# Four-layer graph network on one core: the order of the work around pairs 1 to 3, and where theta's third part is made

## Chip, cores and metric

The kernel runs on one core of one Trainium2 chip. The metric is the device time of one execution in microseconds (us). A core has a matrix engine (TensorE, here PE), a vector engine (VectorE, DVE), an activation engine (ScalarE, ACT), a general engine (GpSimd, POOL) and a queue that issues transfers (SyncE, SP). Each of the engines works through its own instructions in the order in which the program names them, and waits at an instruction until what that one reads is ready; whatever stands behind it waits too.

## What is computed

The input x has 32 batches of 512 nodes with 128 features, and adj is a 512 x 512 matrix. Four layers follow one another; each normalises x over the features, takes the positive part h and adds its result to x. The part of the reference that the change touches is layer 0, and in layer 1 the matrix Theta1:

```python
h = jnp.maximum(_layernorm(x, axis=-1), 0.0)
# layer 0
h0 = jnp.einsum('bnf,fg->bng', h, W[0])
h1 = jnp.einsum('bnf,fg->bng', h, W[1])
A = softmax(where(adj > 0, vals, NEG), axis=1)
out = jnp.einsum('ij,bjg->big', A * M, h0) + jnp.einsum('ij,bjg->big', A * (1.0 - M), h1)
x = x + out + bias                       # M is the identity
# layer 1: hops of h over adj, stacked, times Theta1
x = x + relu(stack([h, h1, h2, h1, h2]) @ Theta1 + bias)
```

Layer 2 has two products with a squared adj, and layer 3 is an attention over the nodes. Neither is touched.

## The kernel before

Batches are worked in 16 pairs, q = 0 to 15. A pair's x is one tile of 128 rows by 2 batches by 4 node blocks by 128 features. For layer 0 each pair goes through these steps:

- **Statistics.** Four `bn_stats` on DVE give mean and variance. There are two ways to a scale `rs` and a shift `sh` from there. `early_stats` (L217) makes them with four small operations on POOL, one of which is a power of -1/2 (L235). `stats_steps` (L239) makes a square root on ACT (L254), a reciprocal on DVE (L256) and two small operations on POOL (L258, L259). `stats_of_two` (L265) does the second for two pairs at once. Pairs 0 to 2 use the first way, pair 3 (`ln3`, L784) and later ones the second.
- **h.** Eight activations on ACT (`normed_steps`, L308), one for each batch and node block.
- **Turning h**, so that features lie on the rows. For pairs 0 to 2 PE transposes it (L330, and `turn_first` L607 for pair 0) and ACT copies it out (L333, L611). From pair 3 on, DVE transposes blocks of 32 (L348), and SP issues four writes to memory (L355) and one read back (L357), `hT`.
- **Diagonal.** `diagonal_of` (L805) multiplies the turned h by A's diagonal on POOL, two operations `hd` (L752). `own_sums` (L811) multiplies `hd` by W[0] on PE, 16 matmuls (L817).
- **Projection.** `project_steps` (L461) multiplies the turned h by W[1] on PE, 16 matmuls (L446), and splits the result into three parts: `g_high` on ACT (L468), `g_low` on DVE (L470), `g_mid` on POOL for the first batch (L474) and on DVE for the second (L472).
- **Product.** `mixed` (L820) multiplies a part of g by the same part of the off-diagonal A, eight matmuls (L824); three parts for each of two halves of the rows, 48 in a pair. `added` (L829) adds the sums to x on DVE; `bias` (L450) adds the bias on POOL.

All of PE, DVE, ACT and POOL follow the program order of the source; the schedule is written by hand. Many helpers are generators, and `go(steps, n)` (L477) runs the next n steps of one, so that its pieces can be laid between others. PSUM has eight banks that the tiles named by `bank` share.

Before the rounds stands a front part (to L738), which makes A by a softmax over rows: `later_rows` and `value_rows` on PE, `softmax_rows` (L680) on DVE and ACT, `scaled_rows` on ACT and POOL, and then A's three parts `att_high`, `att_low` and `att_mid` in two halves (L372 to L390). `first_sums` (L836) then does pair 0's sums and leads in pairs 1 to 3, and `round0(q)` (L886) is one pair's round: own sums of pair q, diagonals and projection of pair q + 1, statistics of pairs q - 1 (for layer 1) and q + 5, h of pair q + 4, turn of pair q + 3.

In `first_sums` the order around pair 1's diagonals is this: own sums of pair 0, h of pair 2, projection of pair 1 with its three parts, the last part of pair 0's product, and only then the diagonals of pair 1.

In layer 1, `fixed_parts` (L416) splits two blocks of theta into a high, a low and a middle part (L418 to L421); the middle part and the subtraction before it are on POOL. `split_up` (L971) splits h of a batch into parts through `moving_parts` (L410), whose low part is on POOL (L413) and whose middle part is on DVE (L414).

Of the kernel before, what the change touches and what calls it, by code (L numbers as in the profile page):

```python
# [9 lines left out]
F32 = mybir.dt.float32  # L10
# [3 lines left out]
AF = mybir.ActivationFunctionType  # L14
# [15 lines left out]
def kernel(  # L30
# [186 lines left out]
    def early_stats(q, *groups):  # L217

        st = stats.tile([P, NT, 2, 3], F32, tag="bn", name=f"bn_{q}", bufs=3)
        sd = stats.tile([P, NT, 2], F32, tag="sd", name=f"sd_{q}", bufs=2)  # L220
        rs = stats.tile([P, NT, 2], F32, tag="rs", name=f"rs_{q}")
        sh = stats.tile([P, NT, 2], F32, tag="sh", name=f"sh_{q}")
        shift[q] = sh.rearrange("p k e -> p (k e)")
        scale[q] = rs.rearrange("p k e -> p (k e)")
        for first, end in groups:
            for k in range(first, end):
                b, t = divmod(2 * k, NT)
                nc.vector.bn_stats(st[:, k].rearrange("p e s -> p (e s)"),
                                   xt[q][:, b, t : t + 2, :].rearrange("p t f -> p f t"))
                yield  # L230
            half = slice(first, end)
            nc.gpsimd.tensor_scalar(sd[:, half], st[:, half, :, 2], 1.0 / D, EPS, OP.mult, OP.add)
            nc.gpsimd.tensor_scalar(sh[:, half], st[:, half, :, 1], -1.0, None, OP.mult)
            yield
            nc.gpsimd.tensor_tensor(rs[:, half], sd[:, half], minus_half[:, half], OP.pow)  # L235
            nc.gpsimd.tensor_mul(sh[:, half], sh[:, half], rs[:, half])  # L236
            yield
# [239 lines left out]
    def go(steps, n=99):  # L477
        for _ in range(n):
            if next(steps, steps) is steps:
                return  # L480
# [63 lines left out]
    for t in range(NT):  # L544
        scores[t] = bank(f"p_later_{t}")
        nc.tensor.matmul(scores[t], ident16, m[:, t, :], start=True, stop=False)
    early = [early_stats(0, (0, 2), (2, 4)), early_stats(1, (0, 4)), early_stats(2, (0, 4))]
    go(early[0], 2)
    middle = prep.tile([P, NT], F32, name="middle")
    nc.vector.tensor_sub(middle, above, pi[:, :NT])  # L550
# [56 lines left out]
    def turn_first(b):  # L607
        p = bank(f"p_hT0_0_{b}")
        for t in range(NT):
            nc.tensor.transpose(p[:, blk(t)], h[0][:, b, t, :], ident)  # L610
        nc.scalar.copy(hT[0][:, :, b, :].rearrange("p b (a c) -> p b a c", c=QR), crossed(p))  # L611
# [56 lines left out]
    def later_rows(t):  # L668
        for kk in range(NK):
            nc.tensor.matmul(scores[t], at_row[:, kk, blk(t)], at_col[:, kk, :], start=False, stop=(kk == NK - 1))  # L670

    def value_rows(t):
        pv = bank(f"p_val_{t}")
        for kk in range(NK):
            for i in range(3):
                nc.tensor.matmul(pv, at_row[:, kk, blk(t)], at_part[:, i, kk, :], start=(kk == 0 and i == 0),
                                 stop=(kk == NK - 1 and i == 2))
        scores[t] = scores[t], pv

    def softmax_rows(t, between=lambda: None):  # L680
        ph, pv = scores[t]
        u = us[t]
        nc.vector.scalar_tensor_tensor(u, ph, elastn, att[:, t, :], OP.mult, OP.add)
        between()
        nc.vector.tensor_tensor_reduce(u, pv, u, 1.0, 3.0e38, OP.add, OP.min, least[:, t : t + 1])
        nc.scalar.activation(u, u, AF.Exp, bias=least[:, t : t + 1], scale=-1.0,
                             accum_out=total[:, t : t + 1])

    def inverse(t):
        nc.vector.reciprocal(total[:, t : t + 1], total[:, t : t + 1])  # L690
# [14 lines left out]
    softmax_rows(0)  # L705
    go(project[0][0])
    later_rows(2)
    value_rows(1)
    softmax_rows(1, lambda: inverse(0))
    scaled_rows(0)  # L710
    go(early[1], 1)
    later_rows(3)
    value_rows(2)
    turn_first(1)
    value_rows(3)

    def inverted(t):
# [5 lines left out]
    next(project[0][1])  # L723
    softmax_rows(3, lambda: inverted(2))
    next(project[0][1])
    go(early[1], 1)
    inverse(3)
    pt = [[bank(f"p_attT_{half}_{j}") for j in range(2)] for half in range(2)]
    transpose_rows(0)
# [1 line left out]
    att_high(0, 0, False)  # L731
    att_high(1, 0, True)
    scaled_rows(3)
    go(early[1], 1)
    go(project[0][1])
    go(early[1])
    att_low(0)
# [43 lines left out]
            yield  # L781

    ahead = {q: stats_steps(q, apart=True) for q in (4, 5)}
    ln3 = stats_steps(3, apart=True)  # L784
    own, turning, hd, adiag = {}, {}, {}, []
    sums_ahead = late_parts()

# [17 lines left out]
    def diagonal_of(q, b):  # L805
        hd[q, b] = straight(turned_of(q), b, adiag[0], f"hd_{q}_{b}")
# [4 lines left out]
    def own_sums(q, ps, first):  # L811


        for I, p in enumerate(ps):
            for i in range(2):
                for b in range(2):
                    nc.tensor.matmul(p[:, (2 * i + b) * D : (2 * i + b + 1) * D], hd[q, b][:, blk(2 * I + i)], w0[:, 0, :],  # L817
                                     start=(first and i == 0 and b == 0), stop=not first, skip_group_check=True)
# [17 lines left out]
    def first_sums():  # L836


        adiag.append(region0.tile([P, N], F32, name="adiag", bufs=1))
        ps = opened_sums(0)  # L840
        mixed(0, 0, ps[0], 0, True)
        transpose_rows(2)
        transpose_rows(3)
        p_adiag = bank("p_adiag")
        for t in range(NT):
            nc.tensor.matmul(p_adiag[:, blk(t)], ones, diag[:, t, :], start=True, stop=True)
        att_high(0, 1, True)
        att_high(1, 1, True)
        nc.scalar.copy(adiag[0], p_adiag)
        diagonal_of(0, 0)  # L850
        diagonal_of(0, 1)
        go(normal[1])
        mixed(0, 0, ps[0], 1, True)
        mixed(0, 0, ps[0], 2, True)
        mixed(0, 1, ps[1], 0, True)
        att_low(1)
        mixed(0, 1, ps[1], 1, True)
        go(early[2])
        att_mid(1)
        next(turned[1])  # L860
        go(turned[1])
        own_sums(0, ps, False)
        go(normal[2])
        next(project[1])
        go(project[1])
        mixed(0, 1, ps[1], 2, True)
        diagonal_of(1, 0)
        diagonal_of(1, 1)
        begun[1] = opened_sums(1)
        own_sums(1, begun[1], True)  # L870
        bias(1)
        for I in range(2):
            added(0, I, ps[I])
        next(turned[2])
        go(ln3)
        go(turned[2])
        normalise(3)
        diagonal_of(2, 0)
        diagonal_of(2, 1)
        go(ahead[4], NT)  # L880
        go(turn(3))
        go(ahead[4])
# [3 lines left out]
    def round0(q):  # L886

        more = q + 1 < NQ
        nothing = iter(())
        both = stats_of_two(q - 1, q + 5) if q + 5 < NQ else stats_steps(q - 1, apart=True)  # L890
        ps = begun.pop(q, None)
        if ps is None:
            ps = opened_sums(q)
            own_sums(q, ps, True)
        normal_of = normals.pop(q + 3, nothing)
        go(normal_of)
        go(both, NT)
        if more:
            if q > 1:
                diagonal_of(q + 1, 0)  # L900
                diagonal_of(q + 1, 1)
            steps = projection(q + 1)
            if q != 2:
                next(steps)
                if q > 2:
                    bias(q + 1)
                go(steps)
        if q + 5 >= NQ:
            go(both)
        if q == 1:  # L910
            bias(2)
            normalise(4)
            go(ahead[5])
            h[5] = normed_tile(5)
            normals[5] = normed_steps(5, h[5])
        elif q + 4 < NQ:
            h[q + 4] = normed_tile(q + 4)
            normals[q + 4] = normed_steps(q + 4, h[q + 4])
            go(normals[q + 4], NT)
        if q >= 5:  # L920
            go(sums_ahead, 1)
        for part in range(3):
            mixed(q, 0, ps[0], part, False)
        if q + 3 < NQ:
            go(turn(q + 3))
        if q == 2:
            go(steps)
            bias(q + 1)
        go(both, NT + 1)
        added(q, 0, ps[0])  # L930
        go(both)
        if q in (3, 4):
            next(squares)
            next(squares)
        if q == 5:
            go(squares)
        for part in range(3):
            mixed(q, 1, ps[1], part, False)
        added(q, 1, ps[1])
        if q == NQ - 1:  # L940
            own[q] = stats_steps(q)
        if q % 2 and q // 2 + NQ // 4 < NQ // 2:
            loads(q // 2 + NQ // 4)

    def layer1(more, square):
# [84 lines left out]
        yield  # L1030
        pair = small_tile("th_high", F32R), small_tile("th_low", F32R)
        th_parts = pair[0][:, : 2 * D], pair[0][:, 2 * D :], pair[1][:, : 2 * D]
        fixed_parts(th[:, 0:2, :].rearrange("p k f -> p (k f)"), *th_parts)
        split_up(0, 0)
        split_up(0, 1)
        split_up(1, 0)
        normalised(2)
# [519 lines left out]
```

## Time and profile before

| what | us |
|---|---|
| median of 3 runs | 885.37 (885.09 to 885.38) |
| profiled execution, whole time | 884.78 |
| its span, first to last instruction | 883.0 |
| PE busy from 0 to 20, 20 to 40, 40 to 60 | 16.64, 17.56, 16.19 |
| PE busy from 60 to 120 | 60.00 |
| PE busy from 120 to 200, 200 to 270 | 79.70, 69.61 |
| PE busy from 270 to 600, 600 to 883 | 330.00, 279.06 |
| DVE and POOL busy from 66 to 110 | 40.09, 40.52 |

In lines of the profile, L12 is line 12 of the source. A line of a timeline has the start, the duration, the engine, the line, the operation, and what it writes and reads; several of the same kind are drawn together (x8). A line of the waits has who waited for whom, then the total in us, how often, and the longest. The mean clock that PE was granted is 0.998 of full.

### The profile page before, as it was taken

The page shows a single profiled execution, that of the slowest core. Times are in us where ns is not written, and L with a number is a line of the kernel's source. Part 1 is how long each engine was busy: PE and PEld are TensorE (multiplying, and loading weights), DVE is VectorE, ACT ScalarE, POOL GpSimd, SP SyncE. Part 2 cuts the span into 40 slices and gives each one's busy share as a digit, 9 for nine tenths or more (in the row PEclk, how much of TensorE's full clock was granted, in tenths as well). Part 3 has the DMA queues.
Part 4 walks back from the last instruction along what each step waited for, and adds up shares of the span by engine and source line. Part 5 has one row for each costly group of instructions (what it writes and reads, how often), then busy time and mean ns, then how long its engine had stood idle before and what let it go on. Part 6 is the DMA issues. An engine that isn't in the chain of part 4 may idle for free.

```text
span 883.0 us, 16282 instructions
## 1 busy us (share of the span) xinstructions
PE 868.8 (98%) x5528; PEld 771.6 (87%) x5528; DVE 700.5 (79%) x1412; ACT 576.7 (65%) x1282; POOL 607.4 (69%) x625
## 2 busy tenths in 40 slices
PE   8799999999999999999999999999999999999998
PEld 4699999988888888888888888888889888899987
DVE  7769876568687787788778888888789789988875
ACT  5765565356555655556666888875688778766674
POOL 6659988767677767867776566565376766677664
PEclk9999999999999999999999999999999999999999
DMA  9137664312322213122332445455445555545442
GB/s 257 34 103 208 193 190 120 96 49 72 98 70 72 73 48 96 49 69 75 97 112 80 120 123 143 140 146 148 137 120 144 156 155 159 149 143 148 120 108 85
DMA packets 107684, 103.91 MB, mean 118 GB/s; under 512 B 9552, under 2 KB 94160, under 8 KB 107600
## 3 DMA queue, kind: packets, MB, share of 16 engines
q1 hardware_dynamic: 107312, 102.34, 40.7%
q8 instruction: 44, 0.72, 0.4%
q10 hardware_dynamic: 288, 0.52, 0.2%
q14 instruction: 40, 0.33, 0.1%
HBM read 53.02 MB, written 49.81 MB: 116 GB/s over the span
## 4 chain that ended last, share of the span: by engine, by line
PE 93%; POOL 2%; DVE 2%; ACT 2%; issue 1%; DMA 1%; SPq 0%; POOLq 0%; ACTq 0%
PE p_av L1324 13%; PE p_l L1016 10%; PE p_hidden L1220 10%; PE p_x1T L397 10%; PE p_l L824 10%; PE p_score L1302 10%; PE p_w L995 5%; PE p_l L446 3%; PE p_z L446 3%; PE p_l L817 3%; PE p_g L446 3%; PE p_w L997 3%; PE p_feat L1197 3%; PE p_hidden L1200 3%; PE p_query L1256 2%; PE p_hv L1268 2%
## 5 line engine op out<-in xcount | busy, mean ns | idle before, releaser
L1324 PEld LDWEIGHTS p_av<-hv,ex 128*128 128x128 f32 x1024 | 119.2, 191 | 3.0 <-POOL ex L1297 0.4
L1324 PE MATMUL p_av<-hv,ex 128*128 128x129 f32 x1024 | 119.6, 274 | 0.2 <-POOL ex L1297 0.2
L1297 POOL TENSOR_TENSOR ex<-ex,adjTx 128x512 f32<-128x512 f32 x64 | 100.2, 1584 | 6.9 <-issue 3.5
L1297 DVE TENSOR_TENSOR ex<-ex,adjTx 128x512 f32<-128x512 f32 x64 | 79.4, 1243 | 32.1 <-ACT ex L1295 30.7
L427 POOL TENSOR_TENSOR key<-key 128x512 fp32r<-128x512 f32 x32 | 47.4, 1480 | 83.5 <-DVE key L426 65.2
L312 ACT ACTIVATE h<-x,sh,rs 128x128 f32<-128x128 f32 x256 | 102.9, 482 | 1.0 <-POOL sh L236 0.9
L1126 ACT ACTIVATE h<-x,sh,rs 128x128 f32<-128x128 f32 x256 | 102.9, 484 | 0.0
L413 POOL TENSOR_TENSOR low_h<-h,high_h 128x512 fp32r<-128x512 f32 x32 | 55.4, 1734 | 45.3 <-PE p_w L997 29.6
L1303 ACT ACTIVATE ex<-p_score 128x512 f32<-128x512 f32 x128 | 76.2, 598 | 11.7 <-PE p_score L1302 4.7
L1295 ACT ACTIVATE ex<-ex 128x512 f32<-128x512 f32 x128 | 77.3, 634 | 0.0
L1184 POOL TENSOR_SCALAR high_hT<-hT 128x512 fp32r<-128x512 f32 x32 | 20.7, 646 | 55.9 <-PE p_hidden L1200 27.1
L245 DVE BATCH_NORM_STATS2 bn<-x 128x6 f32<-128x256 f32 x160 | 58.3, 419 | 0.0
L399 ACT COPY x1T<-p_x1T 128x512 f32<-128x512 f32 x32 | 18.8, 587 | 57.7 <-PE p_x1T L397 57.7
L1240 POOL TENSOR_TENSOR x<-x,phi2b 128x256 f32<-128x256 f32 x64 | 56.2, 897 | 0.0
L413 POOL TENSOR_TENSOR low_hs<-hs,high_hs 128x512 fp32r<-128x512 f32 x32 | 44.1, 1389 | 15.1 <-ACT high_hs L412 14.5
L1302 PE MATMUL p_score<-high_query,key 128*128 128x512 f32 x128 | 50.5, 394 | 0.0
L1302 PE MATMUL p_score<-low_query,key 128*128 128x512 f32 x128 | 50.4, 394 | 0.0
L1302 PE MATMUL p_score<-mid_query,key 128*128 128x512 f32 x128 | 50.4, 394 | 0.0
L431 ACT ACTIVATE high_query<-p_query 128x512 fp32r<-128x512 f32 x32 | 19.2, 601 | 46.4 <-PE p_query L1256 46.4
L997 PE MATMUL p_w<-th,x1T 128*128 128x128 f32 x256 | 49.0, 273 | 0.0
L414 DVE SCALAR_TENSOR_TENSOR mid_h<-h,high_h 128x512 fp32r<-128x512 f32 x32 | 27.9, 877 | 23.5 <-ACT high_h L412 15.1
L432 DVE SCALAR_TENSOR_TENSOR z<-p_z,z 128x512 fp32r<-128x512 f32 x31 | 21.4, 691 | 30.3 <-ACT z L431 30.3
(250 smaller groups left out, 2642.4 us busy)
## 6 DMA issues: line engine op xcount, KB each, us to landing
d<-hb SPq DMA_DIRECT2D x128, 128.0 KB, 2.4
hT<-d SPq DMA_DIRECT2D x32, 512.0 KB, 3.8
d_hT<-hb_hT SPq DMA_DIRECT2D x116, 128.0 KB, 2.4
hT<-d_hT SPq DMA_DIRECT2D x29, 512.0 KB, 3.2
x<-in_x_dram SPq DMA_DIRECT2D x32, 256.0 KB, 5.0
dv<-hvb SPq DMA_DIRECT2D x128, 64.0 KB, 1.8
hvt<-dv SPq DMA_DIRECT2D x32, 256.0 KB, 2.6
out_dram<-x SPq DMA_DIRECT2D x31, 256.0 KB, 2.5
```

Source lines behind the costliest of these rows:

```text
L312: nc.scalar.activation(h[:, b, t, :], xt[q][:, b, t, :], AF.Relu, bias=shift[q][:, i : i + 1], scale=scale[q][:, i : i + 1])
L397: nc.tensor.matmul(p, right[part][:, blk(t)], left[part][:, t, :], start=(t == 0 and part == 0), stop=(t == NT - 1 and part == 2))
L413: nc.gpsimd.tensor_sub(low, x, high.bitcast(F32))
L446: nc.tensor.matmul(p[:, blk(t)], hT(t), w, start=(i == 0), stop=(i == len(terms) - 1))
L824: nc.tensor.matmul(p[:, i * 2 * D : (i + 1) * 2 * D], att_parts[part][:, t, blk(2 * I + i)], g[q][part][:, t].rearrange("p b f -> p (b f)" ...
L1016: nc.tensor.matmul(p, adj_parts[part][:, t, blk(i)], w[r][part][:, t, :], start=(part == 0 and t == 0), stop=(part == 2 and t == NT - 1))
L1126: nc.scalar.activation(h[:, t, :], xt[q][:, b, t, :], AF.Relu, bias=shift[q][:, i : i + 1], scale=scale[q][:, i : i + 1])
L1220: nc.tensor.matmul(sums2[n], weighed_features[n][i][:, blk(t)], sq[i][:, t, :], start=False, stop=(i == 2 and t == NT - 1), skip_group_che ...
L1295: nc.scalar.activation(ex[:, t, :], ex[:, t, :], AF.Exp, scale=8.0)
L1297: eng.tensor_mul(split(ex[:, t, :]), split(ex[:, t, :]), crossed(mask[:, t, :]))
L1302: nc.tensor.matmul(p, keys[n][i][:, t, :], query[n][i], start=(i == 0), stop=(i == 2))
L1324: nc.tensor.matmul(po[:, i, : D + 1], ex[:, t, blk(i0 + i)], hv[:, t, :], start=(t == 0), stop=(t == NT - 1))
```

## The change

It has five parts.

In the front, `turn_first(1)` goes from behind `value_rows(2)` to ahead of `value_rows(1)`. Of the four `bn_stats` of pair 1, which stood one by one among the softmax's steps (L711, L722, L726, L734), the first goes into `softmax_rows(1)`, the second stays at L722, and the third joins the fourth behind `scaled_rows(3)`.

Pair 3's statistics go from `stats_steps` (root on ACT, reciprocal on DVE) to `early_stats` (power on POOL), and stand behind h of pair 2.

In `first_sums` the diagonals of pair 1 go from behind the last part of pair 0's product to directly behind pair 0's own sums, ahead of h of pair 2 and of the projection of pair 1. Four of the eight activations that make h of pair 3 go ahead of the copies of pair 2's turned h, and the other four stay behind them.

In `round0(1)` two of the three parts of pair 1's product of the first half go ahead of the projection of pair 2.

In layer 1, theta's middle part goes behind the first `split_up`.

```diff
@@ front
-    early = [early_stats(0, (0, 2), (2, 4)), early_stats(1, (0, 4)), early_stats(2, (0, 4))]
+    early = [early_stats(0, (0, 2), (2, 4)), *(early_stats(q, (0, 4)) for q in (1, 2, 3))]
...
     later_rows(2)
+    turn_first(1)
     value_rows(1)
-    softmax_rows(1, lambda: inverse(0))
+
+    def counted():
+        inverse(0)
+        go(early[1], 1)
+
+    softmax_rows(1, counted)
     scaled_rows(0)
-    go(early[1], 1)
     later_rows(3)
     value_rows(2)
-    turn_first(1)
     value_rows(3)
...
     next(project[0][1])
-    go(early[1], 1)
     inverse(3)
...
     scaled_rows(3)
-    go(early[1], 1)
+    go(early[1], 2)
     go(project[0][1])
     go(early[1])
@@ first_sums
-    ln3 = stats_steps(3, apart=True)
...
         own_sums(0, ps, False)
+        diagonal_of(1, 0)
+        diagonal_of(1, 1)
         go(normal[2])
+        go(early[3])
         next(project[1])
         go(project[1])
         mixed(0, 1, ps[1], 2, True)
-        diagonal_of(1, 0)
-        diagonal_of(1, 1)
         begun[1] = opened_sums(1)
         own_sums(1, begun[1], True)
         bias(1)
         for I in range(2):
             added(0, I, ps[I])
         next(turned[2])
-        go(ln3)
+        h[3] = normed_tile(3)
+        normal_3 = normed_steps(3, h[3])
+        go(normal_3, NT)
         go(turned[2])
-        normalise(3)
+        go(normal_3)
         diagonal_of(2, 0)
@@ round0
-            if q != 2:
+            if q > 2:
                 next(steps)
-                if q > 2:
-                    bias(q + 1)
+                bias(q + 1)
                 go(steps)
...
         if q == 1:
+            mixed(q, 0, ps[0], 0, False)
+            mixed(q, 0, ps[0], 1, False)
+            go(steps)
             bias(2)
             normalise(4)
...
-        for part in range(3):
+        for part in range(2 if q == 1 else 0, 3):
             mixed(q, 0, ps[0], part, False)
@@ layer1
-        fixed_parts(th[:, 0:2, :].rearrange("p k f -> p (k f)"), *th_parts)
+        x, (high, low, mid) = th[:, 0:2, :].rearrange("p k f -> p (k f)"), th_parts
+        nc.scalar.activation(high, x, AF.Copy, scale=DOWN)
+        nc.gpsimd.tensor_sub(x, x, high.bitcast(F32))
+        nc.scalar.activation(low, x, AF.Copy, scale=LOW)
         split_up(0, 0)
+        nc.gpsimd.tensor_sub(mid, high.bitcast(F32), low.bitcast(F32))
         split_up(0, 1)
```

## The prediction

> **What bounds the kernel now.** I read the page first: which engine is busy through the span. Then what TensorE (PE) waits for, then the engines' timelines around the longest wait, then the granted clock there.
>
> ```profile
> PE 868.8 (98%) x5528; PEld 771.6 (87%) x5528; DVE 700.5 (79%) x1412; ACT 576.7 (65%) x1282; POOL 607.4 (69%) x625
> PE p_l L817 <- POOL hd L752: 4.5, 2, 3.8
> PE p_l L824 <- DVE att_high L378: 1.5, 1, 1.5
> PE p_x1T L397 <- POOL low_h L413: 0.3, 1, 0.3
> ```
>
> PE carries the span: 883.0 - 868.8 = 14.2 us is all that it is idle, about 4 of it at the end. The change adds no matmul and removes none, so it can act only through the stalls. One is large: the own sums of pair 1 wait 4.5 us for the two diagonal products `hd`. The timelines of PE, POOL and ACT there (start, duration, and in brackets the idle time before):
>
> ```profile
> 37.84 1.19 PE L824 MATMUL p_l<-g_mid,att_mid 128*128 128x256 f32 x8
> 42.83 0.49 PE L817 MATMUL p_l<-w,hd 128*128 128x128 f32 x2 [3.79 <-POOL hd L752]
> 44.06 3.29 PE L817 MATMUL p_l<-w,hd 128*128 128x128 f32 x14 [0.74 <-POOL hd L752]
> ...
> 35.57 0.21 POOL L236 TENSOR_TENSOR sh<-sh,rs 128x8 f32<-128x8 f32 x1
> 40.28 1.27 POOL L474 TENSOR_TENSOR g_mid<-g_high,g_low 128x512 fp32r<-128x512 f32 x1 [4.50 <-DVE g_low L470]
> 41.52 2.49 POOL L752 TENSOR_TENSOR hd<-hT,adiag 128x512 f32<-128x512 f32 x2
> ...
> 34.12 1.07 ACT L333 COPY hT<-p_hT 128x512 f32<-128x512 f32 x2 [0.20 <-PE p_hT L330]
> 35.81 3.19 ACT L312 ACTIVATE h<-x,sh,rs 128x128 f32<-128x128 f32 x8 [0.62 <-POOL sh L236]
> 38.91 1.06 ACT L468 ACTIVATE g_high<-p_g 128x512 fp32r<-128x512 f32 x2
> 39.98 1.28 ACT L254 ACT_TABLE_LOAD   x1
> ```
>
> The input of `hd`, the turned h of pair 1, lies ready at 35.19 (34.12 + 1.07), and POOL is free at 35.78, yet POOL idles 4.50 us: its queue holds `g_mid` in front, which waits for DVE's `g_low`, that for ACT's `g_high`, and that for eight normalisations. The wait is one of order, not of work. It has a second price, in the granted clock:
>
> ```profile
> 43.00:44.00 1.00, 0.32 (x2) 0.87 0.00 0
> 44.00:45.00 1.00, 0.94 (x4) 0.50 0.00 0
> 45.00:46.00 1.00, 1.00 (x7) 0.50 0.00 0
> 46.00:47.00 1.00, 1.00 (x7) 0.50 0.00 0
> ```
>
> The third column from the right is the clock: half speed for some 3.2 us after the gap.
>
> **What the Trainium skill says.** "TensorE: Matmul & The Clock Gate", Part 1, gives an idle window of about 3.4 us after which the clock falls to one half, until a window of work has passed. The trace agrees: 3.79 us idle, then 0.50; the idle 1.47 us before 26.81 leaves 1.00. "ScalarE: Activation LUTs", What ACT_TABLE_LOAD costs, has 1283 ns for a load; here it is 1.28 us. "DMA: Bandwidth & Descriptors", Anatomy of one DMA, has a fixed cost near 2 us, for transfers that GpSimd issues; here SP issues them, and of the transfers that turn h, the trace has 2.4 us for a write and 3.1 to 3.3 for the read back, which I use.
>
> **The change, part by part.**
>
> *1. The front (16 to 34 us): nearly nothing.* Turning batch 1 of pair 0 ahead of `value_rows(1)`, its copy ahead of the second exponential, and pair 1's first bn between the inverse and the minimum delay this minimum by one bn pitch (0.34), and the exponential with it, from 21.05 to 21.39. ACT no longer has the copy (22.38, 0.46 pitch) in its middle: from 22.84 on it is 0.1 early (22.84 + 0.34 - 0.46 = 22.72). The second bn stays where it was. The `att_high` that PE waits for follows this chain: PE starts at 26.67, not 26.81. But two bns (0.34 each) now run behind `att_high`, where one did: DVE goes 25.95 + 0.58 (att_high) + 0.68 (two bns) + 1.19 (g_low, g_mid), so `att_low` starts at 28.40, not 28.20. Its second half is there at 29.70, when PE wants it; that of `att_mid` at 30.90, wanted at 30.66. So 0.24 of stall against 0.14 gained: PE ends these parts at 31.62 instead of 31.56. Bounds -0.1 to 0.5, the latter if each product waits for both halves at once. Pair 1's power stays behind the last `scaled_rows`; `sh` comes at 30.5, h of pair 1 is done at 33.8, and PE's turn, at 33.54, ends at 34.4 as before.
>
> *2. Diagonals in front, pair 3's statistics by a power.* POOL: pair 2's statistics begin at their last bn (33.4) and take the 2.45 us that 33.32 to 35.78 shows: 35.9; then both diagonals until 38.4. PE gets to these sums at 38.9 (turn 33.54, 0.87; own sums 1.79; projection 1.70; product 0.96). So the 4.5 us go, with 0.4 to spare, and with them the half clock: the own sums take 1.79 as at 34.35 and not 3.62 (42.83 to 47.19 less the 0.74); turn, projection and next product take 0.35 less.
> What is moved behind: pair 3's four small POOL steps, 2.45 with the power at 1.67, end at 40.85; `g_mid` of pair 1 waits for them, to 42.1 (41.5 before), but is wanted at 45.1. The Sqrt with its table load moves from 39.98 to behind pair 3's h, 45.2 to 46.5: it lay beside idle time and now is on ACT's chain.
>
> *3. Pair 2's projection inside pair 1's product.* After the turn of pair 2 (PE done at 41.5) its copies stand on ACT behind four of pair 3's h (40.9 to 42.5) and end at 43.05 and 43.55. PE runs two parts of pair 1's product meanwhile (to 43.44), so the projection starts with no wait and ends at 45.14. The same work is done at 52.26 in the kernel before (50.27 + 1.03 + 0.96). PE is now 7.1 us ahead: 4.8 of waits and 2.2 of clock, less 0.1 from part 1, and 0.2 of pipeline fill that the idle column doesn't count. If the copies came late, the cover is gone at once: each us late is a us.
>
> *4. Who is late next.* From here PE is 7.1 ahead, and the helpers must be too. Before, this was the room:
>
> ```profile
> 56.70 0.34 SPq L357 DMA_DIRECT2D hT<-d_hT  x1
> 60.76 1.95 PE L446 MATMUL p_g<-w,hT 128*128 128x128 f32 x16
> ...
> 62.85 0.34 SPq L357 DMA_DIRECT2D hT<-d_hT  x1
> 67.21 1.95 PE L446 MATMUL p_g<-w,hT 128*128 128x128 f32 x16
> ```
>
> With 3.2 for the landing: 59.9 for 60.76, and 66.05 for 67.21, so 0.9 and 1.2 us. Pair 3: h complete at 45.2, DVE's turn at 45.95, and 7.2 from there (52.72 to 59.9): 53.15, for PE at 53.65. It fits. Its diagonals on POOL come behind pair 6's statistics: ACT's table load, pair 4's h (47.9 to 51.1), DVE's turn of pair 4 (to 53.45), bn, Sqrt, inverse, then 55.95 to 58.45, for PE at 58.23: 0.2 late. Pair 4's h lands at 53.45 + 7.0 = 60.45, for PE at 60.24: 0.2 late. Then ACT, DVE and POOL are some 5.3 us ahead of before, PE 6.7; from 66 to 95 us DVE and POOL are busy over 90% and do not catch up, but the rooms there are larger (pair 5's h 2.0, read at 71.37 and used at 76.54; pair 6's 3.7; pair 5's diagonals 3.9, done at 80.2 and used at 84.08); only pair 4's diagonals, with 1.3, cost about 0.1. SP's queue keeps its order: the loads of four x stand between pair 4's read and pair 5's writes as before. Step 4 costs 0.5, bounds 0 to 3: the chain has some 20 steps with 0.1 of doubt each, and PE pays as soon as it is late.
>
> *5. theta's mid.* POOL's 0.74 us step goes behind the first `low_h`, on which PE waits 0.30 at 186.27. The low part may start up to 1.2 us earlier if the memory under its tile is free; before, the step in its way waited itself for a PE product. Bounds -0.1 and 0.3; I take 0.2 gained. DVE's `mid_h` beside it is no nearer to PE than before.
>
> Sum: -7.1 + 0.5 - 0.2 = -6.8. The doubts of step 4 are one-sided, so I take 0.3 off: -6.5. The profiled execution took 884.78 (span 883.0), which gives 878.3; it lies 0.6 below the median of 885.37, from which it is 878.9. I forecast the median.
>
> **Rivals.**
> - *The chain of helpers holds it.* ACT's load, the statistics and the two turns by DMA give pairs 3 and 4 another 2 to 3.5 us of waits. For: rooms of 0.9 and 1.2 us, and DVE and POOL loads over 90%. Against: the sum puts each helper about 5 us ahead of before. Time 885.37 - 6.8 + 2 to 3.5 = 880.6 to 882.1, say 881.4.
> - *It doesn't do what it says*: the diagonals are still late at 39 us because pair 2's power ends later, or the gap comes back whole at pair 3. Room is only 0.4; but a miss costs its own size unless it passes 3.4 us. Then 4.5 and 2.2 are paid elsewhere: 885.3.
> - *Slower*: h of pair 3 comes by DMA so late that PE idles at its projection over the clock's window. Its own wait then adds 2.2 of half clock. It turns slower when the landing, 53.15 in my sum, comes after 53.65 + 7.1 - 2.2 + 1.8 = 60.35, later than in the kernel before (59.9); for that pair 3's statistics would have to be 7 us late behind POOL's power. At 61.4 it is 7.75 of idle and 2.2, less 7.1: 888.2. Against: all its steps have rows here.
>
> **How the numbers follow.** This kernel's runs lie within 0.03%; 0.2%, or 1.8 us, is what can be told from no change: below 883.6 or above 887.1. Forecast (877.6 to 880.3): 0.64, at 878.9. Helpers hold it: 0.22, at 881.4, nearly all below 883.6. Gap stays: 0.09, at 885.3. Slower: 0.05. So faster 0.86, same 0.09, slower 0.05. The low end, 877.6, is step 4 at nothing, the 0.3 not taken off, the 0.1 of part 1 won and theta's whole 0.3, with what the runs scatter; the high end, 882.4, takes in most of the second case; about 0.18 is left outside.
>
> **What would show it.** Right: no L817 wait on `hd` near 39 us, clock 1.00 from 30 to 60, the projection of pair 2 ending near 45.1, PE's waits from 29 to 62 below 1.5 us in all, and a table load near 45. Wrong: a wait of PE on `hT` or `hd` of pairs 3 and 4 over 1 us, a clock below 1 between 40 and 70, or layer 1's first product (184.88 before) starting less than 5 us earlier.

## The result and the profile after

The changed kernel takes 878.59 us in the median of four runs (877.80 to 879.01), the kernel before 885.23 (884.54 to 885.38). The ratio is 0.9926, with a 95% interval from 0.9908 to 0.9943. The profiled execution took 878.54, with a span of 876.8.

The page of the kernel after, busy time of the engines:

```profile
PE 867.1 (99%) x5528; PEld 770.3 (88%) x5528; DVE 702.2 (80%) x1411; ACT 576.2 (66%) x1281; POOL 607.8 (69%) x627
```

PE is idle for 9.7 us, where it was 14.2, and busy for 1.7 us less with the same 5528 matmuls, most of it because none runs at half clock any more. Together these are the 6.2 us of the span. The medians differ by more, 6.6 us: most executions of the kernel before have a lower mean clock than its profiled one; more on this stands at the experiment without the diagonals. What PE waits for after the change (who for whom, total us, times, longest):

```profile
...
PE p_l L826 <- DVE att_high L378: 1.1, 1, 1.1
PE p_g L446 <- DMA hT<-d_hT: 0.6, 1, 0.6
...
PE p_x1T L397 <- POOL low_h L413: 0.2, 1, 0.2
```

The 4.5 us on `hd` are gone. PE's timeline there, in the kernel after (start, duration; no bracket means no wait):

```profile
38.71 1.95 PE L819 MATMUL p_l<-w,hd 128*128 128x128 f32 x16
40.50 1.04 PE L330 MATMUL p_hT<-ident,h 128*128 128x128 f32 x8
41.29 1.20 PE L826 MATMUL p_l<-g_high,att_high 128*128 128x256 f32 x8
42.33 1.12 PE L826 MATMUL p_l<-g_low,att_low 128*128 128x256 f32 x8
43.28 1.95 PE L446 MATMUL p_g<-w,hT 128*128 128x128 f32 x16
44.99 1.20 PE L826 MATMUL p_l<-g_mid,att_mid 128*128 128x256 f32 x8
```

Pair 2's projection, with two parts of pair 1's product ahead of it, ends at 44.99. In the kernel before, the projection came first, and the same work ended at 52.26:

```profile
48.46 2.05 PE L446 MATMUL p_g<-w,hT 128*128 128x128 f32 x16 [0.24 <-ACT hT L333]
50.27 1.20 PE L824 MATMUL p_l<-g_high,att_high 128*128 128x256 f32 x8
51.30 1.12 PE L824 MATMUL p_l<-g_low,att_low 128*128 128x256 f32 x8
52.26 1.12 PE L824 MATMUL p_l<-g_mid,att_mid 128*128 128x256 f32 x8
```

The helpers that make this possible, POOL first and then ACT, in the same execution:

```profile
35.57 2.50 POOL L755 TENSOR_TENSOR hd<-hT,adiag 128x512 f32<-128x512 f32 x2
38.63 1.67 POOL L235 TENSOR_TENSOR rs<-sd,minus_half 128x8 f32<-128x8 f32 x1
40.38 0.21 POOL L236 TENSOR_TENSOR sh<-sh,rs 128x8 f32<-128x8 f32 x1
40.54 1.28 POOL L474 TENSOR_TENSOR g_mid<-g_high,g_low 128x512 fp32r<-128x512 f32 x1
...
40.62 1.65 ACT L312 ACTIVATE h<-x,sh,rs 128x128 f32<-128x128 f32 x4 [0.82 <-POOL sh L236]
42.17 1.04 ACT L333 COPY hT<-p_hT 128x512 f32<-128x512 f32 x2
43.12 1.65 ACT L312 ACTIVATE h<-x,sh,rs 128x128 f32<-128x128 f32 x4
44.78 1.28 ACT L254 ACT_TABLE_LOAD   x1
```

The diagonals are done at 38.07, 0.6 us before PE reads them. The first copy of pair 2 is done at 42.7, also 0.6 us before PE wants it. The table load now stands in the middle of ACT's work. The clock (third column from the right) stays whole:

```profile
38.00:42.00 4.00, 4.00 (x38) 1.00 0.00 0
42.00:46.00 4.00, 4.00 (x37) 1.00 0.00 0
```

### The profile page after: what moved, and what is told of

Same layout as the page of the kernel before. It is cut to its first block, busy times and chain, and to the rows that moved or that the text cites. A ratio compares the mean times of both kernels' runs of the same rounds, so it can differ in the third digit from the quotient of the medians.

```text
span 876.8 us, 16276 instructions
## 1 busy us (share of the span) xinstructions
PE 867.1 (99%) x5528; PEld 770.3 (88%) x5528; DVE 702.2 (80%) x1411; ACT 576.2 (66%) x1281; POOL 607.8 (69%) x627
## 4 chain that ended last, share of the span: by engine, by line
PE 86%; DVE 5%; POOL 2%; ACT 2%; DMA 2%; SPq 1%; issue 1%; DVEq 0%; POOLq 0%; ACTq 0%
PE p_av L1335 13%; PE p_l L1023 10%; PE p_hidden L1231 10%; PE p_x1T L397 10%; PE p_score L1313 10%; PE p_l L826 5%; PE p_w L1002 5%; PE p_l L446 3%; PE p_z L446 3%; PE p_w L1004 3%; PE p_feat L1208 3%; PE p_hidden L1211 3%; PE p_query L1267 2%; PE p_hv L1279 2%; PE p_g L446 2%; PE p_l L819 1%
## 5 line engine op out<-in xcount | busy, mean ns | idle before, releaser
L1002 PE MATMUL p_w<-th_high,high_hs 128*128 128x256 f32 x128 | 45.4, 354 | 0.0
L1146 DVE STREAM_TRANSPOSE hb<-h 128x512 f32<-128x512 f32 x64 | 43.5, 696 | 2.3 <-DMA d<-hb 1.7
```

Of the source, the lines that this page charges most:

```text
L1002: nc.tensor.matmul(p, hs_parts[q, b][part][:, blk(t)], th_parts[part], start=(part == 0 and t % 2 == 0), stop=False, skip_group_check=True)
```

## The experiments

Times are medians; "before" is the kernel before in runs on the same chip at the same time, 885.33 for the first four experiments, 884.93 for the next four, 885.17 for the last three.

**Wait and clock apart.** Ahead of pair 1's own sums in the kernel before:

```diff
+        idle = bank("p_fill")
+        for _ in range(14):
+            nc.tensor.matmul(idle, att_parts[0][:, 0, blk(0)], att_parts[0][:, 0, :], start=True, stop=True)
         begun[1] = opened_sums(1)
```

> The kernel before, with 14 more products of 512 columns on PE (thrown away) in the stall ahead of pair 1's own sums. Theory: the stall has two prices, 4.8 us of waiting and 2.2 us of half clock; 14 x 0.23 = 3.3 us of filler fit into the 4.0 us gap, the waits end when they did (hd done at 42.8 and 44.0), but the clock stays at 1.00: 885.2 - 2.2 = 883.0, own sums 14 matmuls in 1.6 instead of 3.3 us. Rival: the half clock has another cause than the gap, it stays at 0.50 and the time at 885.2 or above.

Measured: 884.32, ratio 0.9990 (0.9984 to 0.9997). PE's timeline of this kernel:

```profile
38.88 3.36 PE L871 MATMUL p_fill<-att_high 128*128 128x512 f32 x14
42.89 0.49 PE L817 MATMUL p_l<-w,hd 128*128 128x128 f32 x2 [0.64 <-POOL hd L752]
44.11 1.83 PE L817 MATMUL p_l<-w,hd 128*128 128x128 f32 x14 [0.73 <-POOL hd L752]
45.77 1.04 PE L330 MATMUL p_hT<-ident,h 128*128 128x128 f32 x8
...
60.18 2.02 PE L446 MATMUL p_g<-w,hT 128*128 128x128 f32 x16 [0.68 <-DMA hT<-d_hT]
```

The waits end where they did and the clock stays at 1.00, in all 20 runs at 0.999 or more in the mean, so the gap is the cause of the half clock. Its price in the profiled executions is smaller than expected: from 44.11 to the start of what follows, the fourteen matmuls take 1.66 us (to 45.77), against 3.13 (44.06 to 47.19) before. That is 1.5 us, not 2.2. PE is 1.4 ahead until pair 3's projection. There 0.7 is lost: pair 3's writes are issued 1.4 earlier than before, but took 5.2 us here (51.46 to 56.67) against 3.8 (52.88 to 56.70), so the read back is issued no earlier. Why they took longer isn't known.

**The diagonals alone.** In the kernel before:

```diff
         own_sums(0, ps, False)
+        diagonal_of(1, 0)
+        diagonal_of(1, 1)
...
         mixed(0, 1, ps[1], 2, True)
-        diagonal_of(1, 0)
-        diagonal_of(1, 1)
```

> The kernel before with only the diagonals of pair 1 moved behind pair 0's own sums. Theory: the wait on hd goes, but PE then stands at pair 2's projection, since ACT's copies of its turned h lie behind pair 3's Sqrt, which lies behind four bns (about 43.9): copies from 44.3, PE there at 41.4, wait 3.0 to 3.5. Time 882, or 884 if this wait takes the clock down. Rival (the move of the diagonals alone is the whole gain): 879.

Measured: 881.26, ratio 0.9961 (0.9946 to 0.9976). The wait moves to the next place, as PE's timeline of this kernel shows:

```profile
40.75 1.04 PE L330 MATMUL p_hT<-ident,h 128*128 128x128 f32 x8
44.87 2.05 PE L446 MATMUL p_g<-w,hT 128*128 128x128 f32 x16 [3.08 <-ACT hT L333]
```

ACT stands at pair 3's root until 44.04, and pair 2's copies lie behind it. Some 4 of the change's 6.6 us come from this edit alone, the rest only with help. Three of its four runs (880.90 to 881.27) have a mean clock of 1.0; the fourth, with 883.65, has 0.996. So the clock still goes down in some executions and not in others. The wait of 3.1 us is the longest one left, but that it is the cause isn't shown, since the profile is of an execution at 1.0.

**All but the order of projection and product.**

```diff
-            if q > 2:
+            if q != 2:
                 next(steps)
-                bias(q + 1)
+                if q > 2:
+                    bias(q + 1)
...
         if q == 1:
-            mixed(q, 0, ps[0], 0, False)
-            mixed(q, 0, ps[0], 1, False)
-            go(steps)
             bias(2)
...
-        for part in range(2 if q == 1 else 0, 3):
+        for part in range(3):
```

> The changed kernel with pair 2's projection ahead of pair 1's whole product again. Theory: PE is at the projection at 41.3, the first copy is there at 42.8: 1.4 us of wait and nothing that gives it back, 880.0. Rival (the order of projection and product is of no account, since something later holds PE): 878.6.

Measured: 879.80, ratio 0.9937 (0.9920 to 0.9954), with a wait of 1.29 us on pair 2's copies at 42.73. As expected: it is 1.2 us more than the changed kernel, about what the wait says, though the intervals of the two ratios overlap.

**All but pair 3's statistics.**

```diff
+    ln3 = stats_steps(3, apart=True)
...
-        go(early[3])
...
-        h[3] = normed_tile(3)
-        normal_3 = normed_steps(3, h[3])
-        go(normal_3, NT)
+        go(ln3)
         go(turned[2])
-        go(normal_3)
+        normalise(3)
```

> The changed kernel with pair 3's statistics by the root on ACT again, at the old place, and its h whole behind the copies. Theory: the root waits for bns that end at about 43.9, copies from 44.3: PE waits 1.5 us at pair 2's projection (43.3), and pair 3's h is turned 3.5 us later, landing at 56.3, for PE at 55.1: 1.2 more. 881.3. Rival (power instead of root only exchanges equal work): 878.6.

Measured: 883.61 (16 runs, 881.88 to 885.92), ratio 0.9981 (0.9973 to 0.9988), more lost than expected. PE's timeline has both waits that were named, and the second is larger:

```profile
44.68 2.05 PE L446 MATMUL p_g<-w,hT 128*128 128x128 f32 x16 [1.22 <-ACT hT L333]
...
57.84 2.02 PE L446 MATMUL p_g<-w,hT 128*128 128x128 f32 x16 [2.62 <-DMA hT<-d_hT]
```

Pair 3's writes again took 5.2 us (49.10 to 54.30), which is the extra 1.4. The five runs with a mean clock of 0.999 or 1.0 take 881.88 to 882.92, the eleven below that 883.3 to 885.9, so in many executions the clock goes down as well. Which wait takes it down isn't shown, since the one execution that was profiled is at 1.0.

**All but the diagonals.**

```diff
         own_sums(0, ps, False)
-        diagonal_of(1, 0)
-        diagonal_of(1, 1)
...
+        diagonal_of(1, 0)
+        diagonal_of(1, 1)
         begun[1] = opened_sums(1)
```

> The changed kernel with the diagonals of pair 1 back behind the last part of pair 0's product. Theory: POOL then has pair 3's power and g_mid ahead of them: g_mid from 40.5, diagonals 41.2 to 43.7; PE at these sums at 38.7 waits 5 us, the clock falls to one half, 7 us lost, 885.5: the other parts bring nothing without this one. Rival (each part is worth something alone): 882 to 883.

Measured: 885.16 against 884.93, ratio 1.0003 (0.9995 to 1.0012). The old wait stands where it stood:

```profile
42.82 0.80 PE L819 MATMUL p_l<-w,hd 128*128 128x128 f32 x2 [3.81 <-POOL hd L755]
44.04 3.36 PE L819 MATMUL p_l<-w,hd 128*128 128x128 f32 x14 [0.43 <-POOL hd L755]
```

It is no longer than before, although pair 3's power now stands ahead of `g_mid` on POOL: POOL was done with it at 38.3 and still idled 2 us for `g_low`. In this detail the expectation was wrong. The main point holds: without the diagonals in front the other parts bring nothing.

The clock of this execution shows something that the profile of the kernel before does not:

```profile
42.00:46.00 4.00, 2.75 (x11) 0.53 0.00 0
46.00:50.00 4.00, 4.00 (x24) 0.62 0.00 0
```

If PE ran at 0.50 or at 1.00, as elsewhere in these profiles, that is some 6.8 us at half clock. In the profile of the kernel before it is 3.4 (0.87 in the microsecond from 43, 0.50 in the next three, 0.92 in that from 47), after a gap of the same length (3.79 us, and 3.81 here). The eight transposes behind the own sums, from 47.19 to 48.76, take 1.57 us instead of the 0.79 of the changed kernel (40.50 to 41.29). The mean clock goes with it: 0.996 here, 0.998 in the profile of the kernel before. Of the 59 runs of the kernel before that stand beside the experiments, 42 have 0.995 or 0.996. In the first 35 of them these took 885.4 in the median, those at 0.998 took 884.7. So in most executions, as far as the mean clock tells, the half clock costs more than the 1.5 us of the profile.

**The front as before.**

```diff
     later_rows(2)
-    turn_first(1)
     value_rows(1)
...
-    softmax_rows(1, counted)
+    softmax_rows(1, lambda: inverse(0))
     scaled_rows(0)
+    go(early[1], 1)
     later_rows(3)
     value_rows(2)
+    turn_first(1)
     value_rows(3)
...
+    go(early[1], 1)
     inverse(3)
...
-    go(early[1], 2)
+    go(early[1], 1)
```

> The changed kernel with the front (turn of pair 0, bns of pair 1) as before. Theory: the front part is worth nothing: -0.1 to +0.2, PE's products with att_mid end at the same time within 0.2. 878.6. Rival (the front is part of the gain): 879.5 or above, waits of PE on att_high 1.5 and not 1.1.

Measured: 878.64, ratio 0.9927 (0.9912 to 0.9942). PE waits 1.46 us for `att_high` instead of 1.12, and from there to pair 0's own sums it takes 7.53 us instead of 7.87. The two cancel.

**What comes next.** Pair 3's power done twice, the same values:

```diff
-            nc.gpsimd.tensor_tensor(rs[:, half], sd[:, half], minus_half[:, half], OP.pow)
+            for _ in range(2 if q == 3 else 1):
+                nc.gpsimd.tensor_tensor(rs[:, half], sd[:, half], minus_half[:, half], OP.pow)
```

> The changed kernel with pair 3's power done twice on POOL (same values, 1.67 us more). Theory: the chain statistics, h of pair 3, copies of pair 2 is what comes next: PE has the copy of pair 2 some 0.5 us early (42.77 for 43.28), so about 1.1 us of wait appear there, and pair 3's turned h (52.7 for 53.56) is late by less than that again: 879.7. Rival (room is 1.7 or more): 878.6; other rival (pair 3's transfer adds its own delay): 880.5 or above.

Measured: 880.28 (879.63 to 881.26), ratio 0.9947 (0.9932 to 0.9962); the profiled execution took 879.63. PE's timeline of this kernel:

```profile
44.56 2.05 PE L447 MATMUL p_g<-w,hT 128*128 128x128 f32 x16 [1.09 <-ACT hT L334]
...
61.89 2.02 PE L447 MATMUL p_g<-w,hT 128*128 128x128 f32 x16 [0.34 <-DMA hT<-d_hT]
```

Of 1.67 us more on POOL, 0.6 is hidden and 1.1 is waited for at the copies, as expected. The second wait is at pair 4's transfer and not at pair 3's. The profiled execution is 1.1 us slower than that of the changed kernel, the median 1.7.

**The wait on pair 9.** SP's timeline in the kernel after: the transposed adj (L500) and four loads of x (L135) stand ahead of pair 9's writes and read.

```profile
89.32 3.72 SPq L500 DMA_DIRECT2D adjT_d<-adj_squares  x4
93.08 3.80 SPq L135 DMA_DIRECT2D x<-in_x_dram  x4
96.98 2.32 SPq L355 DMA_DIRECT2D d_hT<-hb_hT  x4
103.49 0.34 SPq L357 DMA_DIRECT2D hT<-d_hT  x1
```

```diff
-        if q == 5:
+        if q == 6:
             go(squares)
```

> The changed kernel with the transfers of the turned adj one round later (round 6 in place of 5). Theory: PE's one wait on a transfer, 0.56 us at 107.5 for pair 9's turned h, comes from SP's queue, where these four and the loads of four x stand ahead of pair 9's writes; moved behind them, the read is issued some 3 us earlier and the wait goes: 0.5 to 0.7 less, 878.0. Rival (the wait is from the load of the DMA engines, whatever the order): the wait stays or moves to another pair, 878.6.

Measured: 878.76, ratio 0.9928 (0.9914 to 0.9943), with no wait on pair 9 in the profile. That doesn't decide it. The kernels with the old front and with the change repeated keep the old order, and their profiles have no such wait either: from pair 1's own sums to layer 1's first product PE takes 139.88 us in the first profile of the changed kernel, 139.33 here, and 139.15 and 139.29 in those two. The wait comes and goes between executions. What differs is how long pair 9's four writes take, from the first one's issue to the read's: 6.5 us in the first profile (96.98 to 103.49), 5.6 in that of the change repeated (97.15 to 102.75), 5.9 with the old front (97.17 to 103.04). They are issued at the same time within 0.2 us, so between these executions the time of the writes decides, and not their place in SP's queue.

**The changed kernel again, and a better one.** The last three ran together. First the changed kernel as it is:

> The changed kernel once more, unchanged, for what its own executions scatter by. Theory: two small waits come and go between executions of one program: 0.6 us on a transfer for pair 9, and 1.0 us at the start of layer 2, where a DVE operation of 0.68 us takes 1.85 us when a POOL operation[...] began first (0.68 in three of these kernels' profiles and 1.85 in four, though the program there is the same). Times from 877.3 to 879.3 in two or three heaps. Rival: one heap, 878.6.

Then with `mid_hT` earlier:

```diff
             weighed(C, 1)
+            if last:
+                more("split")
             go(late_stats)
...
+        elif step == "split":
+            go(entering["split"])
```

> The changed kernel with the first mid_hT of layer 2 ahead of the reciprocal and the product of the statistics on DVE. Theory: it then always meets POOL's running operation (from 422.76) and always waits for its end at 424.04, is done at 424.7, as in the good case, and PE (424.85) never waits: the upper heap goes, 0.3 to 0.6 less in the median, 878.1. Rival: the two statistics operations now meet the POOL operation, and hold what follows by the same: 878.6 or above.

And with this and the later transfers of the turned adj:

> Both: the transfers of the turned adj one round later and mid_hT earlier. Theory: neither wait is left, 877.5 to 877.8, and the scatter under 0.8. Rival: 878.6, the waits turn up elsewhere.

Measured: 878.33 (878.25 to 879.20; ratio to before 0.9925, interval 0.9912 to 0.9937), 878.10 (878.00 to 878.47; 0.9919, 0.9906 to 0.9933) and 877.68 (877.57 to 878.29; 0.9915, 0.9902 to 0.9929). The unchanged kernel's five runs lie in two heaps: 878.25 to 878.33 and 879.17 to 879.20. DVE's and POOL's timelines show the coin that is tossed. In the first profile of the changed kernel:

```profile
424.00 0.68 DVE L1198 SCALAR_TENSOR_TENSOR mid_hT<-hT,high_hT 128x512 fp32r<-128x512 f32 x1
...
422.76 5.58 POOL L1017 TENSOR_TENSOR hs<-hs,b 128x512 f32<-128x512 f32 x4
```

In the profile of the same kernel run again:

```profile
423.64 1.85 DVE L1198 SCALAR_TENSOR_TENSOR mid_hT<-hT,high_hT 128x512 fp32r<-128x512 f32 x1
...
422.39 5.49 POOL L1017 TENSOR_TENSOR hs<-hs,b 128x512 f32<-128x512 f32 x4
```

In both, DVE's operation starts some 1.24 us after POOL's first, just where POOL's second begins. If DVE is first it takes 0.68; if not, it stands until POOL's second is done and takes 1.85, and PE waits 0.6 us for it. From layer 2's first product to layer 3's first score this costs 0.9 us (203.60 against 202.70). With `mid_hT` moved:

```profile
422.60 1.52 DVE L1200 SCALAR_TENSOR_TENSOR mid_hT<-hT,high_hT 128x512 fp32r<-128x512 f32 x1
```

It now starts inside POOL's first operation, waits for its end, and is done at 424.12, in time for PE, which reads it at 424.57. The upper heap is gone, in these five runs and in the four of the kernel with both edits. The kernel with both edits has the lowest median of all. Its intervals overlap those of the changed kernel, so the 0.65 us between them are seen but not settled.

## Why the prediction was right

It gave 878.9 with a range from 877.6 to 882.4; the median is 878.59. It was right in what it said of the mechanism: the wait on `hd` was one of order, and once the diagonals stood in front it went, with the half clock. That the median is so close is in part luck. The sum was made on one profiled execution, from 884.78 to 878.3, and that came to 878.54, a gain of 6.2 for the 6.5 of the forecast. The median gained 6.6, which fits that most executions of the kernel before lose more to the half clock than the profiled one; the forecast didn't reckon with that. By its steps:

1. *The front, nearly nothing.* Right in the sum; both terms were larger than forecast. PE waits 0.35 less for `att_high` (0.14 in the forecast) and takes 0.33 longer from there to the own sums (0.2), and the kernel with the old front has the same time.
2. *Diagonals in front.* Right: the sums start at 38.71 (38.9 in the forecast) with 0.6 to spare (0.4). The experiment without this edit gives the old time.
3. *Projection inside the product.* The end is right: 44.99 for 45.14, with no wait. The split of the 7.1 us into 4.8 of waits and 2.2 of clock was off for the execution that it was read from. The filler shows the clock at 1.5 there. The remaining 0.7 belongs to the waits, though their idle column doesn't count it: in the filler kernel, at full clock, the own sums take 2.15 us outside their second wait (42.89 to 45.77, less 0.73) against 1.79 without one, and turn and projection take as long as before (3.08 us, 45.77 to 48.85). It doesn't touch the sum, which was taken from end to end.
4. *Who is late next.* The size is right, the place isn't. The forecast had 0.5 us of waits at pair 3's and 4's diagonals and at pair 4's transfer. There are none there: the helpers were up to 0.7 us quicker than in the sum (pair 4's h starts at 47.33, not 47.9), and PE's sums and projections at 48.91, 53.56, 58.23 and 60.06 have no bracket. In the profiled execution the 0.6 came at pair 9, for which the forecast looked at no room: 1.4 us before (read issued at 109.22, 3.2 to land, PE at 113.84). Pair 9's writes are issued 7.0 us earlier than before, as far ahead as PE, but take 6.5 us to the read instead of 5.2 (104.00 to 109.22), so the read is only 5.7 ahead.
5. *theta's mid.* Mis-sized. The wait on `low_h` fell from 0.30 to 0.17, but from layer 1's first product to layer 2's first PE takes 246.01 us, against 246.03 before. The filler kernel and the one with the diagonals alone, with the old theta, have 246.02 and 246.00. The room was thought to be in POOL's queue; in the profile after, ACT's `high_h` itself waits 1.21 us for a PE product. It starts at 177.83, 0.76 ahead of layer 1's first product, where before it started 1.72 ahead (183.16 for 184.88). So `low_h` starts at 178.54, 0.05 ahead of that product where it was 0.05 behind. Why `high_h` now waits for a later product isn't known, and no run had this edit alone.

Of the rivals, "the chain of helpers holds it" was the near miss: of 1.67 us more in that chain (power done twice), 0.6 found room and the rest was paid at once, 1.1 us in the profiled executions. "It doesn't do what it says" is what the kernel without the diagonals does. "Slower" was far off: even with pair 3's read issued 4.8 us later (54.30 for 49.49), as in the kernel with the root, the time stays below that of the kernel before.

The Trainium skill was borne out on the clock: "TensorE: Matmul & The Clock Gate", Part 1, calls the window free-running, and the traces agree that a gap of one length has no fixed price: 3.79 us gave 3.4 us at half clock in the profile of the kernel before, 3.81 gave 6.8 in that of the kernel without the diagonals, and runs of the kernel before alone have mean clocks from 0.995 to 0.998.

## What to carry to other kernels

Before a wait is put down to a slow engine, look at whether its input was ready and its engine free: here POOL idled for 4.5 us with the input of `hd` ready, and only the order of the queue stood between. An order edit has to be followed until every queue has its new slack; the diagonals alone brought 4 us, the other edits without them nothing, and all together 6.6. And when PE gains, list the room of every later transfer against the new arrival, not only of the next two. And before a price is read from one profile, compare its mean clock with that of the other runs: here the profiled execution of the kernel before was of the cheaper kind.

## What the runs showed of the hardware that had not been expected

A DVE operation with two inputs in SBUF and a POOL operation that reads SBUF held each other up. "SBUF — State Buffer", in SBUF: two separate sides, calls the shared pair of ports an exclusive lock that whoever starts first holds for its whole instruction; the trace agrees (0.68 and 1.85 us for one operation in two executions of one program). New was that a start within hundredths of a microsecond of POOL's next operation makes a program's time fall into two heaps 0.9 us apart, more than the front or theta's part are worth. One gap in PE's work of 3.8 us was followed by 3.4 us at half clock in the profile of one kernel and by 6.8 in that of another. The four writes that turn pair 3's h took 3.8 us in some profiles and 5.2 in others, those of pair 9 between 5 and 6.5, from the first issue to the read's; what sets this was not found.
